# Layer 0's head and linear parts in another order, and two heads' maxima taken from neighbouring PSUM banks

## The chip, the cores and the metric

The kernel runs on one core of one Trainium2 chip. The metric is the device time of one execution in microseconds (us). The core has five engines with queues of their own: PE (TensorE, matmuls; PEld are its weight loads), DVE (VectorE), ACT (ScalarE), POOL (GpSimd) and SP (which issues most DMAs). The 16 KB of PSUM in each partition are eight banks of 512 fp32 numbers; PE writes its results there, and DVE and ACT read them.

## The reference

Two layers over x of 2 x 2048 tokens with 256 features. In each, x is normed, an attention-like part `s` and a feed-forward-like part `g` are computed from the normed x, and x becomes x + s * silu(g).

```
layer 0: s = linear attention(xn): rope, elu + 1 features, sums over all keys, W_out
         g = block(xn): layernorm, 16 causal heads of 16 with rope, Wproj, residual,
             layernorm, top-2 of 8 experts with capacity 1024, gelu, residual
layer 1: s = 16 causal heads of 16 + 16 (real and imaginary), Wo
         g = xn @ int4(kernel) + bias + (xn @ a) @ b
```

Softmax of the causal heads subtracts each row's maximum over the keys that the row may see.

## The kernel before

Tokens lie in tiles of 128 rows, 16 for each of two batch entries. The stages are a prelude (constants, loads), the attention of layer 0 with the linear attention and the routing to experts woven into it, the experts, and the attention of layer 1 with the rest of layer 1 woven in.

Heads are worked on in groups of four, eight groups per layer (two batch entries of four). The four heads of a group lie in four bands of 32 partitions, so that four score products run side by side, one in each band of rows of PE. For a group, pass A (`pass_a`) computes scores with queries in the rows, 128 queries by up to 512 keys, only for the row maxima; pass B (`pass_b`) computes them again with keys in the rows, after the maximum has been folded into the queries (layer 0, `subtract`) or added by a product (layer 1, `less_maximum`), and ACT takes the exponential (line 574) into `pt`. The value sums are products in column bands (line 804 in layer 0, line 1557 in layer 1). One step of the loop in `run_attention` takes one block of pass A and one of pass B for all four heads, in two halves of two heads each; a group has 40 blocks of pass A and 36 of pass B.

In pass A, a block that lies fully below the diagonal is reduced by DVE with a plain `tensor_reduce` (line 547). A block that holds the diagonal is reduced by a custom DVE instruction that adds a mask from the constants and takes the maximum (line 543). Each head has a bank and a reduction of its own. In pass B, the diagonal blocks get their mask by `hide` (line 505): four bf16 products of 32 rows, 256 columns wide, that add the mask `mask_h` in PSUM.

The order of the work is planned in Python, when the kernel is built, by the class `Plan`. The kernel declares steps with an engine, an estimated cost, the tiles read and written and a strand ("S" for the scores, "prep", "lin" and so on). Steps of one strand on one engine stay in order; a beam search chooses the order across strands by estimated times, and gives each PSUM tile one of the eight banks (the kind "s"). What is planned is emitted in that order, and the engines follow it with semaphores.

The names that follow in the text are these. `normalise0` norms four tiles of x: moments on DVE (`stats`, lines 476 and 478), a chain of small POOL instructions for the inverse roots (lines 481 to 488), scaling on ACT (line 696). `norm` scales a pair of tiles again for the block's own layernorm into `hn` (ACT, line 717), turns it on PE (line 360) and writes `ht` (DVE, line 721). `project` computes q, k and v of a tile (PE, line 736), copies them to `raw` (ACT, line 755), rotates them on POOL (lines 743 to 757), and after each second tile turns both (PE, line 764) and copies them to `qt` and `kt` (lines 770 and 772). `prepare` lists these parts for a group; the first group's are all declared before the loop, a later group's are spread over the loop's steps of the group before. The linear attention has `lin_keys` and `lin_out`, each over pairs of tiles (their products at lines 1066, 1117 and 1160, their rotation on POOL at lines 1039 to 1045); they fall due every 7.5 steps, from step 0 for the first batch entry and from step 180 for the second. `route` picks the experts and sends the rows on POOL (line 1000).

Of the kernel before, what the change touches and what calls it, by code (L numbers as in the profile page):

```python
# [17 lines left out]
P = 128  # L18
# [14 lines left out]
C_TRI = C_CAUSAL + 512  # L33
# [9 lines left out]
def _constants():  # L43
# [4 lines left out]
    c[:, C_CAUSAL + 384 : C_CAUSAL + 512] = np.where(r[None] <= r[:, None], 0.0, FAR)  # L48
# [23 lines left out]
class Buf:  # L72
# [3 lines left out]
    def __init__(self, kind):  # L76
        self.kind, self.n, self.uses, self.t = kind, None, 0, None
# [9 lines left out]
class State:  # L87


    def __init__(self, plan):  # L90
# [7 lines left out]
        self.since = {k: [0.0] * len(x) for k, x in plan.kinds.items()}  # L98
# [13 lines left out]
class Plan:  # L112
# [15 lines left out]

    GAP = 0.1
# [52 lines left out]
    def places(self, st, strand, s, t):  # L182

        take = []
        for b in s.bufs:
            if st.slot[b.n] is None:
# [3 lines left out]
                taken = [i for x, i in take if x.kind == b.kind]  # L190
                at, n = None, None
                for i, x in enumerate(st.since[b.kind]):
                    if x is not None and (at is None or x < at) and i not in taken:
                        at, n = x, i
# [6 lines left out]
    def advance(self, st, handicaps, until):  # L201
# [3 lines left out]
        while st.todo:  # L205
# [36 lines left out]
            for b, i in take:  # L242
                st.slot[b.n], st.since[b.kind][i] = i, None
                if b.kind == "s" and key[0] != "S":
                    st.guest[b.n] = key[0]
                    st.held[key[0]] = st.held.get(key[0], 0) + 1
# [18 lines left out]
            for b in s.bufs:  # L265
                st.left[b.n] -= 1
                st.until[b.n] = max(st.until[b.n], done)
                if st.left[b.n] == 0:
                    if st.guest[b.n]:
                        st.held[st.guest[b.n]] -= 1  # L270
                    st.since[b.kind][st.slot[b.n]] = st.until[b.n]
        return True

    def run(self):
# [36 lines left out]
        for s, take in order:  # L311
            for b, i in take:
                b.t = self.kinds[b.kind][i]()
# [5 lines left out]
def kernel(ctx: ExitStack, tc: tile.TileContext, i: dict, out: bass.AP):  # L319
# [15 lines left out]
    causal = cst[:, C_CAUSAL : C_CAUSAL + 512]  # L335
# [6 lines left out]
    def load_x(n):  # L342
        s = slice(n * NA // 4, (n + 1) * NA // 4)
        nc.sync.dma_start(xr[:, s], x_in[:, s])
# [32 lines left out]
    w0 = early.enter_context(tc.tile_pool(name="w0", bufs=1))  # L377
    prelude = ctx.enter_context(ExitStack())
# [6 lines left out]
    load_x(0)  # L385
# [4 lines left out]
    load_x(1)  # L390
# [4 lines left out]
    load_x(2)  # L395
    load_x(3)
# [4 lines left out]
    for n, c in enumerate((C_ID, C_AFTER)):  # L401
# [9 lines left out]
        if n == 0:  # L411
            nc.vector.tensor_copy(ident_h, m)
        else:
            nc.vector.tensor_copy(mask_h, m[:, :, None].to_broadcast([P, 4, 2, P]))
# [32 lines left out]
    def banks(ps, names):  # L447
        return [lambda n=n: ps.tile([P, 512], F32, tag=n, name=n, bufs=1) for n in names]
# [52 lines left out]
    def hide(out, j):  # L501

        r = slice(32 * j, 32 * j + 32)
        for q in range(4):
            nc.tensor.matmul(out, ident_h[r, q], mask_h[r, q].rearrange("p n k -> p (n k)"), start=False, stop=q == 3)  # L505
# [8 lines left out]
    def run_attention(plan, make, prepare, subtract, sum_keys, finish, last_sum, before=None, others=(), between=False):  # L514
# [16 lines left out]
        def pass_a(g, t, k, j, w, mx, parts):  # L531

            s, r, out = Buf("s"), slice(32 * j, 32 * j + 32), (mx, t, k, j)

            def score():
                nc.tensor.matmul(  # L536
                    s.t[:, :w], g.qt.t[r, t * P : (t + 1) * P], g.kt.t[r, 512 * k : 512 * k + w], start=True, stop=True
                )

            def largest():  # L540
                to = mx.t[:, t % 2, j, k : k + 1]
                if k == t // 4:
                    nc.vector.tensor_tensor_reduce(  # L543
                        s.t[:, :w], s.t[:, :w], causal[:, 512 - w :], 1.0, -3e38, ALU.add, ALU.max, to
                    )
                else:
                    nc.vector.tensor_reduce(to, s.t[:, :w], AX.X, ALU.max)  # L547

            keys = range(4 * k, 4 * k + -(-w // P))
            step = S("S", "PE", t_row(w), score, r=[(g.qt, t), *((g.kt, n) for n in keys)], w=[s], on=j)  # L550
            S("A", "DVE", t_dve(w) + (0.19 if k == t // 4 else 0.0), largest, r=[s], w=[out])
            parts.append(out)
            return step

        def pass_b(g, c, p, j, pt):
# [11 lines left out]
            def rest():  # L567
                if before:
                    S("S", "PE", 0.25 * t_row(w), before(g, c, j, s, w, not diagonal), r=[s, g.mh[c]], w=[s], on=j)
                if diagonal:  # L570
                    S("S", "PE", T_HIDE, lambda: hide(s.t[:, : 2 * P], j), r=[s], w=[s], on=j)
# [10 lines left out]
        for u in range(at + last_sum + 1):  # L582
# [11 lines left out]
            for i in (0, 2):  # L594


                more = []
                for x in range(2):
                    if a:
                        plan.pace = pass_a(g, t, k, i + x, wa, mx, parts)  # L600
                        first = first or plan.pace
                    if b:
                        step, rest, weigh = pass_b(gb, cb, p, (i + 2 + x) % 4, pt)
                        first = first or step
                        more.append((rest, weigh))
                for rest, _ in more:
# [36 lines left out]
    with ExitStack() as sc:  # L643
# [13 lines left out]
        for vt in vts:  # L657
            nc.vector.memset(vt, 1.0)
# [7 lines left out]
        nc.gpsimd.memset(ones, 1.0)  # L666
        outs = {}
# [3 lines left out]
                s=banks(ps, [f"s{n}" for n in range(8)]),  # L671
# [18 lines left out]
        def normalise0(n0):  # L690

            xs = [("xr", n0 + n) for n in range(4)]

            def scale():
                for n in range(n0, n0 + 4):
# [4 lines left out]
            stats("prep", n0, "r", ln_r, ln_m, ln_r1)  # L700
            S("prep", "ACT", 1.5, scale, r=[("r", n0)], w=xs)
# [9 lines left out]
        def norm(G, t):  # L711
# [14 lines left out]
            S("prep", "ACT", 0.75, shrink, r=[("xr", n0), ("xr", n0 + 1), ("r", n0 // 4 * 4)], w=[hn])  # L726
# [3 lines left out]
        def project(G, t):  # L730
# [27 lines left out]
            if t % 2:  # L758
                tp, at = Buf("s"), (t - 1) * P

                def turn():
                    for x in range(2):
                        for n in range(2):
                            nc.tensor.transpose(
# [939 lines left out]
```

## Time and profile before

| | |
|---|---|
| median of 3 runs (lowest, highest) | 3483.42 us (3477.35, 3490.22) |
| the profiled execution's own time, its span | 3508.01 us, 3506.2 us |
| busy share of the span: PE, PEld, DVE, ACT, POOL | 96%, 68%, 62%, 48%, 47% |
| mean granted TensorE clock | 0.97 |
| first score of layer 0, of layer 1 | 31.6 us, 2002.7 us |
| first product of the experts | 1505.28 us |

Rows of the profile name a line, an engine and an operation, the tile written and the tiles read, shapes as partitions x elements, a count, busy time and mean duration. Idle time is put down to the instruction that released the engine. Matmuls are pipelined and their ends are modelled, so that a busy PE is not PE at its peak; the starts of matmuls are the surer reading. An fp32 product is two matmul instructions.

### The profile page before, as it was taken

How to read it: one execution, taken by the hardware profiler on the slowest of the kernel's cores; microseconds unless marked ns; L12 is line 12 of the kernel's file. 1: busy time of each engine (PE TensorE's matmuls, PEld its weight loads, DVE VectorE, ACT ScalarE, POOL GpSimd, SP SyncE). 2: the span in 40 equal slices, each digit the busy share in tenths (PEclk: the TensorE clock that was granted, in tenths of full speed). 3: DMA queues.
4: the chain of work that ended last, by engine and by line, in shares of the span. 5: the costliest groups of instructions: out<-in, count | busy, mean ns of one | idle time of the engine just before them, and what ended most of it. 6: DMA issues, size and time to landing. Idle time of an engine off the chain costs nothing.

```text
span 3506.2 us, 81341 instructions
## 1 busy us (share of the span) xinstructions
PE 3350.0 (96%) x33814; PEld 2373.5 (68%) x33814; DVE 2163.6 (62%) x5599; ACT 1682.6 (48%) x3336; POOL 1660.5 (47%) x2223
## 2 busy tenths in 40 slices
PE   6999999999999999689989999999999999999998
PEld 4767777776777776456666556666776767777775
DVE  4777777777777877421121266667766657666774
ACT  3565555554555554311111265555445554554554
POOL 4443222323332221400000167989876657877877
PEclk7999999999999999789999999999999999999999
DMA  5000000000000000143333221010001010000000
GB/s 181 2 2 2 8 8 8 20 16 26 10 10 5 14 14 12 38 156 113 114 100 113 76 67 45 23 51 29 24 11 36 14 42 17 15 17 21 11 26 25
DMA packets 99508, 133.24 MB, mean 38 GB/s; under 512 B 9395, under 2 KB 76671, under 8 KB 99138
## 3 DMA queue, kind: packets, MB, share of 16 engines
q1 hardware_dynamic: 92994, 114.14, 10.1%
q0 software_dynamic: 6144, 13.88, 1.3%
q8 instruction: 266, 4.36, 0.5%
q14 instruction: 104, 0.85, 0.1%
HBM read 93.15 MB, written 37.75 MB: 37 GB/s over the span
## 4 chain that ended last, share of the span: by engine, by line
PE 45%; POOL 7%; DVE 2%; ACT 1%; issue 1%; DMA 1%; POOLq 0%; ACTq 0%; DVEq 0%
PE s L562 7%; PE s L536 7%; PE s L1347 6%; PE s L1341 6%; PE s L1557 6%; PE s L1468 3%; PE s L1526 2%; POOL ps L1542 2%; PE s L1563 2%; POOL ps L1543 2%; PE s L1605 2%; PE s L1483 1%; POOL ps L1538 1%; PE s L505 1%; PE s L1642 1%
## 5 line engine op out<-in xcount | busy, mean ns | idle before, releaser
L574 ACT ACTIVATE pt<-s 128x512 f32<-128x512 f32 (+1 forms) x2304 | 1168.9, 576 | 713.6 <-PE s L562 249.0
L562 PE MATMUL s<-qt,kt 32*128 32x256 f32 (+1 forms) x9216 | 1292.6, 388 | 7.9 <-ACT pt L574 4.4
L536 PE MATMUL s<-kt,qt 32*128 32x512 f32 (+3 forms) x5120 | 1269.7, 559 | 10.2 <-ACT pt L574 2.3
L547 DVE TENSOR_REDUCE mx<-s 128x1 f32<-128x512 f32 x1536 | 961.5, 682 | 185.0 <-PE s L536 101.9
L562 PEld LDWEIGHTS s<-qt,kt 32*128 32x128 f32 x9216 | 984.6, 185 | 62.0 <-ACT pt L574 16.2
L536 PEld LDWEIGHTS s<-kt,qt 32*128 32x128 f32 x5120 | 530.0, 186 | 170.0 <-issue 94.2
L543 DVE CUSTOM_DVE_ANT_0 s<-s,cst 128x128 f32<-128x128 f32 (+3 forms) x1024 | 482.3, 513 | 120.0 <-PE s L536 82.9
L1538 POOL TENSOR_TENSOR ps<-pt 128x1024 f32<-128x1024 f32 (+1 forms) x160 | 344.5, 2153 | 144.7 <-ACT pt L574 118.5
L743 POOL TENSOR_TENSOR ra<-raw,rope 128x128 f32<-128x128 f32 x128 | 58.6, 458 | 671.0 <-ACT raw L755 604.7
L1542 POOL TENSOR_TENSOR ps<-ps,pt 128x1024 f32<-128x1024 f32 x128 | 303.7, 2373 | 85.9 <-ACT pt L574 80.8
L1526 PE MATMUL s<-mh,ones_h 3*128 3x512 bf16 (+1 forms) x1152 | 317.3, 367 | 0.7 <-ACT mh L1519 0.7
L804 PE MATMUL s<-pt,vt 128*32 128x256 f32 (+1 forms) x4608 | 280.7, 381 | 5.3 <-issue 4.6
L1543 POOL TENSOR_TENSOR ps<-ps,pt 128x1024 f32<-128x1024 f32 (+1 forms) x128 | 269.2, 2103 | 10.0
L1557 PE MATMUL s<-pt,vt 128*32 128x256 f32 (+1 forms) x4608 | 271.3, 374 | 0.5 <-ACT pt L574 0.3
L1350 DVE TENSOR_TENSOR ye<-s,b 128x256 f32<-128x256 f32 x64 | 27.2, 424 | 391.6 <-PE s L1347 391.6
L1342 ACT ACTIVATE hm<-s,b1c 128x512 f32<-128x512 f32 x128 | 87.9, 687 | 359.6 <-PE s L1341 359.6
L1347 PE MATMUL s<-w,hm 128*128 128x256 f32 x1024 | 226.4, 382 | 8.5 <-ACT hm L1342 8.5
L1341 PE MATMUL s<-xt,w 128*128 128x512 f32 x512 | 226.4, 600 | 8.3 <-DVE xt L1282 8.3
L804 PEld LDWEIGHTS s<-pt,vt 128*32 128x32 f32 x4608 | 136.7, 112 | 135.0 <-issue 31.7
L1557 PEld LDWEIGHTS s<-pt,vt 128*32 128x32 f32 x4608 | 134.3, 110 | 136.4 <-DVE mx L547 18.0
L1347 PEld LDWEIGHTS s<-w,hm 128*128 128x128 f32 x1024 | 196.2, 192 | 42.9 <-ACT hm L1342 8.9
L505 PE MATMUL s<-mask_h,ident_h 32*128 32x256 bf16 x2048 | 197.7, 270 | 1.6 <-issue 1.6
(267 smaller groups left out, 4086.0 us busy)
## 6 DMA issues: line engine op xcount, KB each, us to landing
w<-in_L_ffn_W_dram SPq DMA_DIRECT2D x32, 1024.0 KB, 6.2
gl<-g_dram SPq DMA_DIRECT2D x64, 256.0 KB, 3.0
slots_in<-zero SPq DMA_DIRECT2D x8, 1024.0 KB, 10.2
xe<-slots_in SPq DMA_DIRECT2D x16, 512.0 KB, 8.0
slots_out<-ye SPq DMA_DIRECT2D x16, 512.0 KB, 7.2
xr<-in_L_attn_x_dram SPq DMA_DIRECT2D x4, 1024.0 KB, 5.6
s_dram<-lo SPq DMA_DIRECT2D x16, 256.0 KB, 2.0
hn<-in_L_attn_x_dram SPq DMA_DIRECT2D x16, 256.0 KB, 2.7
```

Of the source, the lines that this page charges most:

```text
L536: nc.tensor.matmul(s.t[:, :w], g.qt.t[r, t * P : (t + 1) * P], g.kt.t[r, 512 * k : 512 * k + w], start=True, stop=True)
L543: nc.vector.tensor_tensor_reduce(s.t[:, :w], s.t[:, :w], causal[:, 512 - w :], 1.0, -3e38, ALU.add, ALU.max, to)
L547: nc.vector.tensor_reduce(to, s.t[:, :w], AX.X, ALU.max)
L562: nc.tensor.matmul(s.t[:, at], g.kt.t[r, kj * P : (kj + 1) * P], g.qt.t[r, QC * c + q0 : QC * (c + 1)], start=n == 0, stop=n == 1 and not ...
L574: S("B", "ACT", t_act(w), lambda: nc.scalar.activation(pt.t[:, j, :w], s.t[:, :w], AF.Exp, scale=0.25), r=[s], w=[(pt, j)])
L804: nc.tensor.matmul(av.t[32 * j : 32 * j + 32, q0:QC], vts[G.vn][:, kj, j], pt.t[:, j, at], start=n == 0, stop=n == len(tiles) - 1,)
L1341: nc.tensor.matmul(ps, w1[:, k, f * P : (f + 1) * P], xt[:, k], start=k == 0, stop=k == 1)
L1347: nc.tensor.matmul(ps[:, :D], hm[:, f, s * P : (s + 1) * P], w2[:, f], start=f == 0, stop=f == FF // P - 1)
L1526: return lambda: nc.tensor.matmul(s.t[:, :w_], ones_h[r], G.mh[c].t[r, 512 - w_ :], start=False, stop=last)
L1538: nc.gpsimd.tensor_tensor(ps.t[:, :, q0:], pt.t[:, :, same], pt.t[:, :, odd], ALU.add)
L1542: nc.gpsimd.tensor_tensor(ps.t, ps.t, pt.t[:, :, even], ALU.add)
L1557: nc.tensor.matmul(av.t[32 * j : 32 * j + 32, q0:QC], G.vt.t[:, kj, j], pt.t[:, j, at], start=n == 0, stop=False)
```

## The change

Six edits come together.

1. In the head, x is loaded in pieces of 2, 2, 12 and 16 tiles, where it was four pieces of 8; `normalise0` takes the first four tiles in two chains of two. The ones in the two `vt` tiles are written by POOL (and only where they are needed), where DVE filled the whole tiles.
2. The turning of q and k leaves `project` for a part of its own, `turned_round`, which `prepare` puts behind the norming of the next pair.
3. The second batch entry's linear parts fall due from step 172, where it was 180.
4. Pass A takes two heads into two neighbouring banks, and one `tensor_reduce` takes both heads' maxima. All eight banks are one PSUM tile, and the planner gives a pair two banks that begin at an even one.
5. In layer 0 the diagonal blocks of pass A get their mask on PE: `hide` with a new bf16 mask `mask_q`, 128 columns wide, four products for each head, and then the joint plain reduction. In layer 1 they keep the custom instruction, head by head. `mask_q` is built in the prelude as the two other tables are; the fp32 mask of 512 columns shrinks to 128 in the constants, and layer 1 builds its own of 512 on POOL.
6. In layer 1 the tile `lt` is there once, where there were two.

```diff
-    load_x(0)
+    load_x(0, 2)
+    load_x(2, 4)
...
-    load_x(1)
+    load_x(4, 16)
...
-    for n, c in enumerate((C_ID, C_AFTER)):
+    for n, c in enumerate((C_ID, C_AFTER, C_CAUSAL)):
...
-    def hide(out, j):
+    def hide(out, j, mask):
         r = slice(32 * j, 32 * j + 32)
         for q in range(4):
-            nc.tensor.matmul(out, ident_h[r, q], mask_h[r, q].rearrange("p n k -> p (n k)"), start=False, stop=q == 3)
+            nc.tensor.matmul(out, ident_h[r, q], mask[r, q], start=False, stop=q == 3)
...
+            s, out, diagonal = Buf("s", True), (mx, t, k, i), k == t // 4
...
+            def products(x):
+                return S("S", "PE", t_row(w), lambda: score(x), r=[...], w=[(s, x)], on=i + x)
+
+            def rest():
+                for x in range(2) if diagonal and causal is None else ():
+                    S("S", "PE", T_HIDE / 2, lambda x=x: hide(s.t[:, x, w - P : w], i + x, mask_q), r=[(s, x)], w=[(s, x)], on=i + x)
+                if diagonal and causal is not None:
+                    for x in range(2):
+                        S("A", "DVE", t_dve(w) + 0.19, lambda x=x: nc.vector.tensor_tensor_reduce(
+                            s.t[:, x, :w], s.t[:, x, :w], causal[:, 512 - w :], 1.0, -3e38, ALU.add, ALU.max,
+                            mx.t[:, t % 2, i + x, k : k + 1],
+                        ), r=[(s, x)], w=[(*out, x)])
...
+                    return
+                S("A", "DVE", t_dve(2 * w), lambda: nc.vector.tensor_reduce(
+                    mx.t[:, t % 2, i : i + 2, k], s.t[:, :, :w], AX.X, ALU.max
+                ), r=[(s, 0), (s, 1)], w=[out])
...
+                if a:
+                    products, after_a = pass_a(g, t, k, i, wa, mx, parts)
                 for x in range(2):
                     if a:
-                        plan.pace = pass_a(g, t, k, i + x, wa, mx, parts)
+                        plan.pace = products(x)
...
+                if a:
+                    after_a()
...
-        for vt in vts:
-            nc.vector.memset(vt, 1.0)
+        for vt in vts:
+            nc.gpsimd.memset(vt[:, :, :, 16:], 1.0)
...
-                    if G.b == 0 and t % 4 == 0:
+                    if G.b == 0 and t == 0:
+                        parts.append(lambda: normalise0(0, 2))
+                        parts.append(lambda: normalise0(2, 2))
+                    elif G.b == 0 and t % 4 == 0:
                         parts.append(lambda t=t: normalise0(t))
                     parts.append(lambda t=t: norm(G, t))
+                if t:
+                    parts.append(lambda t=t - 2: turned_round(G, t))
                 for n in range(2):
                     parts.append(lambda t=t + n: project(G, t))
+            parts.append(lambda: turned_round(G, NT - 2))
...
-            start, every = ((0, 7.5), (180, 7.5))[b]
+            start, every = ((0, 7.5), (172, 7.5))[b]
```

In the planner, a pair is placed where both banks are free, from the time at which the later of them is:

```diff
-                for i, x in enumerate(st.since[b.kind]):
+                for i in range(0, len(since), 2) if b.pair else range(len(since)):
+                    x = since[i]
+                    if b.pair and x is not None:
+                        x = max(x, since[i + 1]) if since[i + 1] is not None else None
```

## The prediction

> **What bounds the kernel now.** I read the page's groups first, then a table of stretches cut where each head group's first score starts, then the timelines of the head, of TensorE and of the tail, then the waits.
>
> ```profile
> 207.70:370.50 162.80, 160.38 (x1808) 115.58 (x1804) 119.10 (x323) 92.07 (x197) 54.74 (x146) 0.97 0.01 2
> 370.50:530.20 159.70, 159.70 (x1884) 121.75 (x1880) 121.48 (x330) 92.51 (x192) 44.54 (x112) 1.00 0.02 8
> 1395.00:1505.00 110.00, 64.20 (x524) 46.70 (x516) 46.52 (x233) 34.79 (x70) 40.74 (x65) 0.74 0.23 76
> ```
>
> Columns: stretch, length, busy PE, PEld, DVE, ACT, POOL, granted clock, DMA share, GB/s. In a settled group of layer 0 (second row) PE is busy throughout and DVE three quarters. Busy PE is not full PE, so I looked at single steps, 4 heads of each pass:
>
> ```profile
> 310.73 0.69 PE L536 MATMUL s<-kt,qt 32*128 32x512 f32 x1
> 311.49 0.49 PE L505 MATMUL s<-mask_h,ident_h 32*128 32x256 bf16 x5
> 313.02 0.42 PE L804 MATMUL s<-pt,vt 128*32 128x256 f32 x4
> 503.66 0.69 PE L536 MATMUL s<-kt,qt 32*128 32x512 f32 x1
> 505.69 0.66 PE L764 MATMUL s<-cst,pad 128*128 128x128 f32 x4
> ```
>
> The step from 503.66 to 505.69 takes 2.03 us; the one from 310.73 to 313.02, whose pass B has mask products (L505) and 128 columns fewer, takes 2.29. Both run without a hole, and 237 of about 300 row stretches in this stage hold one whole step: PE sets the pace there. About 24 stretches hold two or three steps, and these wait for banks, which DVE and ACT empty:
>
> ```profile
> ACT pt L574 <- PE s L562: 247.1, 210, 5.1
> DVE mx L547 <- PE s L562: 64.8, 93, 3.4
> DVE s L543 <- PE s L536: 43.2, 63, 2.2
> PEld s L536 <- DVE mx L547: 11.9, 34, 0.8
> ```
>
> (waits of layer 0's attention: total us, times, longest.) DVE waits for PE much more than PE for DVE. The head is different:
>
> ```profile
> 10.27 1.76 DVE L658 MEMSET vt<- 128x2048 f32 x1 [0.37 <-DVE b1c L420]
> 14.10 1.34 DVE L476 BATCH_NORM_STATS2 ln_st<-xr 128x6 f32<-128x256 f32 x4
> 31.43 0.91 ACT L717 ACTIVATE hn<-xr,ln_n 128x256 f32<-128x256 f32 x2
> 51.33 0.91 ACT L717 ACTIVATE hn<-xr,ln_n 128x256 f32<-128x256 f32 x2 [0.91 <-POOL ln_n L466]
> 60.60 2.09 PE L536 MATMUL s<-kt,qt 32*128 32x512 f32 x8 [0.52 <-DVE qt L770]
> ```
>
> The first score starts at 31.59, and the steps of tiles 4 and 5 wait to 60.60: each pair is normed only after the pair before has been turned and copied.
>
> **The change, part by part** (minus is a gain).
>
> *Head.* A third mask in the prelude: 4 copies of 0.15 us, 8 matmul instructions of 0.23 (16 took 3.73), a cast of 0.69. PE's prelude ends 1.9 us later, and POOL's first memset, which waited for it at 8.85, starts at 10.7. POOL has 2.05 us of memsets and gets two more of 1024 columns (512 took 0.49, so 2.0 us); it is free at 14.7. Queued behind them is the first chain of roots, which started at 15.80 behind DVE's memsets (3.9 us, now gone) and four tiles' moments. With two tiles the chain is 5.5 us for 6.1 (the two-tile power in the tail takes 0.72 for 1.04): `hn` at 20.2 for 21.92. But the chain for tiles 2 and 3 now stands on POOL ahead of the first rotation: that can start at 25.7 for 26.49. First score about 0.8 us earlier. Pair 2 is then normed at 25.7 for 31.43; four rotations of 1.83 end at 33; the next chain, which ran from 45.0 to 51.1 behind a linear part's 4 us of rotation, ends at 39 to 43; the step of 60.60 comes 8 to 12 us earlier. From 95 us PE is busy 110.4 of 112.7, so what is won before that stays won. Check: group 0 takes 176.1 us, groups 1 and 2, with the same linear parts, 162.8 and 159.7, so 14.8 are there to win. I take -11; ends -16 and +2 (POOL's added memsets, nothing else). The small first loads put one more issue (0.6 us on SP) but half the bytes ahead of `wqkv`; POOL's memsets cover both, and uncovered it is that 0.6.
>
> *Maxima of layer 0.* 1024 custom instructions (half of them data, 512 heads) and 768 plain reductions become 256 + 384 joint ones. Four plain ones in a queue take 2.48 us, 0.60 each; custom ones queued take 0.25, 0.38, 0.51 and 0.65 by width, so 0.89 a pair. No joint one is in the trace. The rows of 256 and 512 columns read from PSUM (L813 417 ns, L1569 685 ns) give 149 ns and 1.05 ns a column, less 80 ns of overlap in a queue: 1.14 us for 1024 columns, 0.74 on average for the diagonal ones. Saved: 384 x 0.06 = 23 and 256 x 0.156 = 40, together 63 us of DVE. Since single-step stretches are PE's, I let a quarter come back: -16; ends 0 and -63.
>
> *Maxima of layer 1.* Only the plain ones are joined: 23 us of DVE, a quarter back: -6; ends 0 and -23. The custom ones still run one by one. Building `causal` costs POOL 0.5 us and a copy of 0.25 while PE norms the first tiles; uncovered, 0.8. One `lt` for two: gates are 8 or more parts apart, so no wait.
>
> *Masks of layer 0 on PE.* 512 heads x 4 products of 128 bf16 columns. The 256-column form starts every 0.107 us in its row group, two groups side by side (8 of them from 312.47 to 312.91), so 0.053 each if length decides and 0.107 if the load of weights does: 0.21 to 0.43 us a head, four heads side by side in 128 steps, 27 to 55 us. The two steps above differ by 0.26 where pure length says 0.21; I price a step at 0.26, the nearest row. Steps with 128 or 256 columns have cover: such a step needs 1.07 to 1.28 us of columns and takes at least 1.6 in the trace, waiting for banks. That leaves 64 steps: +17; without cover 128 x 0.26 = +33; ends 0 and +55.
>
> [...] No run here shows the 128-column form.
>
> *Banks.* A pair needs two adjacent free banks, and the first head's bank is held until the joint reduction ends, 0.54 us longer; the second's is free a little sooner. Bounds: nothing, or what the last rival says. I take 0, since one step's eight banks are exactly four pairs.
>
> *Order of turning in other groups, 24 parts for 16:* the same instructions and queues. 0.
>
> *Linear parts 8 steps earlier*, some 33 us. The last one now runs at 1444.7 to 1472.8, within the last two routes: its rotation holds POOL from 1452.10 to 1456.08, the sends come after it, and the last chain of roots starts at 1469.03 though its moments were ready at 1465.43. Moved with it are its rotations (POOL has 67.6 us of work in the 185.8 of group 4, so there is room), its loads of x on SP, and their one `hn` buffer, which group 4's norming may hold until step 174: the first part can lose the two steps, and the rest follow. I take 3.6 us plus some of its 5.9 us of PE: -5; ends -10 and +6 (the same PE work put where PE is full, nothing regained).
>
> *Sum:* -11 - 16 - 6 + 17 + 0 - 5 = -21 us. The profiled execution took 3508.0 (span 3506.2 and 1.8 around it), 24.6 above the median of the runs; I take the difference over: 3483 - 21 = 3462 (3487 under the profiler).
>
> **Rivals.** About 0.5%, 17 us, can be told from no change.
>
> 1. *DVE sets the pace.* For it: stretches of two or three steps take 4.75 us where columns and drain need 3.7, close to DVE's 4.8. Against: only 24 such stretches. Two thirds of the 86 us come back, -57 for -22: 3427. Chance 0.17.
> 2. *The masks eat it.* Nothing covers them: +33 for +17, and the sum is -5: 3478. For it: PE has no hole in 370 to 530 us. Chance 0.15.
> 3. *Pairs of banks (slower).* Prep, linear parts and value sums take single banks out of the pairs, so a pair waits for its second half while the first is empty. Place: the row stretches of both layers. For it: at 1081.9 us a step whose columns need 1.07 us takes 1.98, its second half starting as banks are released. If one step in five of the 640 loses 0.54 us, that is 69 us: 3531. It decides from 38 us on, 71 steps, one in nine. Against: rows and full products alternate, so most steps find empty banks. Chance 0.30.
>
> The forecast has 0.38.
>
> **Numbers.** Faster 0.38 + 0.17 = 0.55, same 0.15, slower 0.30. The range goes down to 3405 (rival 1 and the head's full 16, with some more on banks) and up to 3525 (masks at 55 with nothing from DVE is +39, so 3522, and a milder rival 3).
>
> **What would show it.** Right: first score near 31, and the step of tiles 4 and 5 near 50; group 0 near 165; no custom instruction in layer 0, joint rows of 1.2 us for 1024 columns; 128-column masks starting 0.053 to 0.08 us apart; the last linear part before 1450. Wrong: settled groups of layer 0 longer than 160 us with more PE waits behind L547's successor (rival 3), or the same length with a longer diagonal step (rival 2); layer 1 longer than its 1503 us would be rival 3 alone, for nothing else grows there.

## The result and the profile after

The kernel after takes 3468.99 us (median of 9 runs, 3464.54 to 3474.67), the kernel before 3485.58 (9 runs, 3477.35 to 3494.25): a ratio of 0.9954, 95% interval 0.9941 to 0.9967, or -16.6 us. A second comparison gave 0.9951 (0.9936 to 0.9967). The forecast was -21. Its total is right; the runs below show that most of its terms are not.

The profiled execution of after took 3473.7 us, 4.7 above its median; that of before, 3508.0, lay 24.6 above, and above each of the 37 timed runs of before in the comparisons that gave medians of 3485 to 3488 (the highest took 3494.25). So the two profiles differ by twice what the kernels do, and a stretch that is shorter than in before's profile need not be shorter by as much in a usual run. The stretches that answer to those shown of before (length, busy PE, PEld, DVE, ACT, POOL, clock, DMA share, GB/s):

```profile
205.50:363.40 157.90, 156.86 (x2073) 114.20 (x2069) 111.88 (x181) 92.06 (x198) 55.34 (x147) 1.00 0.01 2
363.40:526.90 163.50, 162.40 (x2146) 123.56 (x2142) 114.09 (x186) 93.33 (x193) 44.70 (x112) 1.00 0.03 8
1383.80:1461.90 78.10, 41.67 (x454) 30.19 (x446) 33.27 (x166) 25.08 (x53) 22.41 (x42) 0.77 0.27 91
```

In the second row, the settled group, DVE is busy for 114.09 us with 186 instructions where it had 121.48 with 330, yet the group is 163.5 us long where it was 159.7. Groups 5 and 6 of layer 0, counted from 0, grew alike (160.0 and 158.3 for 156.5 and 154.8). The stretch between layer 0's last score and the experts (third row) is 78.1 where it was 110.0.

The joint reductions and the new masks in after's groups by form (busy us, mean ns of one, idle before). Line numbers have moved: pass A's products are L548, its maxima L567, pass B's products L581, the masks L514.

```profile
L567 DVE TENSOR_REDUCE mx<-banks 128x2 f32<-128x1024 f32 x832 | 990.4, 1222 | 266.5 <-PE banks L548 131.7 <-PE banks L581 101.0 <-PE banks L514 25.2
L514 PE MATMUL banks<-mask_q,ident_h 32*128 32x128 bf16 x2048 | 109.4, 215 | 0.0
```

A joint reduction of 1024 columns takes 1.222 us in the mean (forecast 1.14; a plain one of 512 took 0.682 in before's mean). A step of 384 columns in TensorE's timeline of after (start, duration), in two halves, of which the first is shown with the start of the second:

```profile
506.15 0.58 PE L548 MATMUL banks<-kt,qt 32*128 32x384 f32 x1 [0.41 <-DVE mx L567]
506.90 0.21 PE L514 MATMUL banks<-mask_q,ident_h 32*128 32x128 bf16 x1
506.96 0.35 PE L514 MATMUL banks<-mask_q,ident_h 32*128 32x128 bf16 x6
507.29 0.58 PE L548 MATMUL banks<-kt,qt 32*128 32x384 f32 x1
```

The second half begins at 507.29, after the masks. In one row group they start at 506.903, 506.959, 507.015 and 507.071: 0.056 us apart with two row groups side by side, the low end of the forecast's 0.053 to 0.107.

The waits of layer 0's attention in after (total us, times, longest):

```profile
ACT pt L593 <- PE banks L581: 196.5, 182, 3.8
DVE mx L567 <- PE banks L581: 138.1, 177, 2.8
DVE mx L567 <- PE banks L514: 47.9, 56, 3.9
PEld banks L548 <- DVE mx L567: 21.2, 66, 0.8
```

DVE's maxima now wait some 215 us for TensorE's scores and masks (the two rows and 28.6 behind L548), where those of before had 147 (64.8 and 29.5 for the plain, 42.3 and 10.8 for the custom ones): DVE was relieved, and the relief became waiting. TensorE's weight loads for pass A wait 21.2 us for the maxima, where they had 11.9 behind the plain and 3.8 behind the custom ones; all its weight loads together wait 36 us for maxima in both kernels. The head, in after's timeline:

```profile
10.27 0.74 DVE L485 BATCH_NORM_STATS2 ln_st<-xr 128x6 f32<-128x256 f32 x2
11.78 1.84 POOL L689 MEMSET vt<- 128x1024 f32 x2
19.24 0.20 POOL L475 TENSOR_TENSOR ln_n<-ln_n,ln_t 128x2 f32<-128x2 f32 x1
22.26 1.09 ACT L721 ACTIVATE xr<-xr,ln_m,ln_r 128x256 f32<-128x256 f32 x2 [4.34 <-POOL ln_m L493]
23.25 0.89 ACT L743 ACTIVATE hn<-xr,ln_n 128x256 f32<-128x256 f32 x2
```

The first root is ready at 19.44, but `hn` starts at 23.25, because ACT's queue holds the scaling of tiles 2 and 3 (22.26) ahead of it, and that waits for the second chain on POOL. The first score is at 34.0, not 31, and the step of tiles 4 and 5 starts at 49.0 (60.6 before). A second profile of after has 32.0 and 47.2.

### The profile page after: what moved, and what is told of

Same layout as the page of the kernel before. It is cut to its first block, busy times and chain, and to the rows that moved or that the text cites. A ratio compares the mean times of both kernels' runs of the same rounds, so it can differ in the third digit from the quotient of the medians.

```text
span 3471.9 us, 84289 instructions
## 1 busy us (share of the span) xinstructions
PE 3326.3 (96%) x35870; PEld 2332.2 (67%) x35870; DVE 2078.6 (60%) x4066; ACT 1678.3 (48%) x3336; POOL 1667.2 (48%) x2242
## 4 chain that ended last, share of the span: by engine, by line
PE 44%; POOL 8%; DVE 2%; ACT 2%; issue 2%; DMA 1%; POOLq 0%; DVEq 0%; ACTq 0%
PE banks L548 7%; PE banks L581 6%; PE s L1381 6%; PE s L1375 6%; PE banks L1594 6%; PE banks L1505 3%; POOL ps L1579 2%; POOL ps L1580 2%; PE banks L1563 2%; PE banks L1600 2%; PE banks L1520 1%; POOL ps L1575 1%; PE banks L1642 1%; PE banks L514 1%; ACT pt L593 1%
## 5 line engine op out<-in xcount | busy, mean ns | idle before, releaser
L593 ACT ACTIVATE pt<-banks 128x512 f32<-128x512 f32 (+1 forms) x2304 | 1165.7, 575 | 713.2 <-PE banks L1563 211.0
L567 DVE TENSOR_REDUCE mx<-banks 128x2 f32<-128x1024 f32 (+3 forms) x1024 | 1121.1, 1122 | 344.5 <-PE banks L581 153.3
L581 PE MATMUL banks<-qt,kt 32*128 32x256 f32 (+1 forms) x9216 | 1247.3, 388 | 8.2 <-DVE mx L567 5.3
L548 PE MATMUL banks<-kt,qt 32*128 32x512 f32 (+3 forms) x5120 | 1239.9, 560 | 11.3 <-DVE mx L567 5.1
L581 PEld LDWEIGHTS banks<-qt,kt 32*128 32x128 f32 x9216 | 935.2, 186 | 44.9 <-ACT pt L593 11.0
L548 PEld LDWEIGHTS banks<-kt,qt 32*128 32x128 f32 x5120 | 486.2, 185 | 205.5 <-issue 111.8
L769 POOL TENSOR_TENSOR ra<-raw,rope 128x128 f32<-128x128 f32 x128 | 60.6, 474 | 540.4 <-ACT raw L781 497.4
L1563 PE MATMUL banks<-mh,ones_h 3*128 3x512 bf16 (+1 forms) x1152 | 299.5, 371 | 0.0
L561 DVE CUSTOM_DVE_ANT_0 banks<-banks,causal 128x384 f32<-128x384 f32 (+3 forms) x512 | 242.4, 514 | 56.8 <-PE banks L548 43.1
L1594 PE MATMUL banks<-pt,vt 128*32 128x256 f32 (+1 forms) x4608 | 275.5, 377 | 0.7 <-ACT pt L593 0.5
L832 PE MATMUL banks<-pt,vt 128*32 128x256 f32 (+1 forms) x4608 | 268.0, 371 | 1.5 <-DVE mx L567 0.9
L1594 PEld LDWEIGHTS banks<-pt,vt 128*32 128x32 f32 x4608 | 135.5, 111 | 141.3 <-ACT pt L593 37.2
L514 PEld LDWEIGHTS <-ident_h 32*128 32x128 bf16 x4096 | 200.0, 93 | 29.6 <-issue 15.1
L832 PEld LDWEIGHTS banks<-pt,vt 128*32 128x32 f32 x4608 | 133.4, 109 | 116.8 <-issue 16.9
```

The lines of the kernel that those rows point to most:

```text
L548: nc.tensor.matmul(s.t[:, x, :w], g.qt.t[r, t * P : (t + 1) * P], g.kt.t[r, 512 * k : 512 * k + w], start=True, stop=not (diagonal and cau ...
L567: S("A", "DVE", t_dve(2 * w), lambda: nc.vector.tensor_reduce(mx.t[:, t % 2, i : i + 2, k], s.t[:, :, :w], AX.X, ALU.max), r=[(s, 0), (s, ...
L581: nc.tensor.matmul(s.t[:, at], g.kt.t[r, kj * P : (kj + 1) * P], g.qt.t[r, QC * c + q0 : QC * (c + 1)], start=n == 0, stop=n == 1 and not ...
L593: S("B", "ACT", t_act(w), lambda: nc.scalar.activation(pt.t[:, j, :w], s.t[:, :w], AF.Exp, scale=0.25), r=[s], w=[(pt, j)])
L832: nc.tensor.matmul(av.t[32 * j : 32 * j + 32, q0:QC], vts[G.vn][:, kj, j], pt.t[:, j, at], start=n == 0, stop=n == len(tiles) - 1,)
L1563: return lambda: nc.tensor.matmul(s.t[:, :w_], ones_h[r], G.mh[c].t[r, 512 - w_ :], start=False, stop=last)
```

## The half clock, which the forecast left out

The granted clock falls to 0.50 at times, in layer 0's groups for 3.4 to 17.1 us (the longest in before, from 49.2 to 66.3 us). The kernel before in stretches of 1 us (the same columns, the clock third from the end):

```profile
265.00:266.00 1.00, 0.00 (x0) 0.00 (x0) 0.26 (x1) 0.00 (x0) 1.00 (x2) 1.00 0.00 0
267.00:268.00 1.00, 1.00 (x5) 0.48 (x4) 1.00 (x3) 1.00 (x4) 0.70 (x3) 0.83 0.00 0
268.00:269.00 1.00, 1.00 (x4) 1.00 (x4) 1.00 (x2) 1.00 (x3) 0.00 (x0) 0.50 0.00 0
277.00:278.00 1.00, 1.00 (x12) 0.20 (x4) 0.00 (x0) 0.00 (x0) 0.00 (x0) 0.55 0.00 0
```

TensorE is idle from 264.9 to 266.8 us and then, from 267.7, has half the clock for 10.2 us: a hole of 1.9 us is followed by a loss of about 5 more. In before's layer 0 six such stretches begin between 70 and 1390 us. The other five (from 677, 735, 804, 855 and 1363 us, 6.8 or 10.2 us long) begin in a route's sends or up to 2.5 us after their end, eight indirect DMAs on POOL in 10.0 to 15.8 us. Two of those in POOL's timeline of before:

```profile
673.68 0.97 POOL L1000 DMA_INDIRECT slots_in<-x,to  x1 [0.30 <-issue]
674.95 0.97 POOL L1000 DMA_INDIRECT slots_in<-x,to  x1 [0.30 <-issue]
```

And the stretches of 4 us around them:

```profile
668.00:672.00 4.00, 4.00 (x44) 2.67 (x46) 3.86 (x17) 1.77 (x4) 3.09 (x4) 1.00 0.41 146
672.00:676.00 4.00, 3.07 (x31) 1.61 (x24) 0.04 (x1) 0.69 (x2) 3.01 (x4) 1.00 0.33 118
676.00:680.00 4.00, 2.93 (x13) 2.11 (x14) 1.51 (x3) 0.87 (x2) 3.21 (x8) 0.66 0.18 66
```

In 672 to 677 TensorE has four gaps, up to 0.91 us, that are put to "issue", and DVE and ACT starve with it. After's profile has none of these stretches in layer 0 between 70 and 1390 us, though its sends are as long (10.0 to 15.8 us for the first five).

The length of a hole doesn't decide it alone. Two runs of the table below, after without edit 5 and the same with layer 1 unpaired, have the same hole in layer 0; in the first the clock stays full, in the second it is halved for 6.8 us. First TensorE's next product and a stretch of 2 us in the one, then in the other:

```profile
778.23 0.66 PE L367 MATMUL banks<-cst,x 128*128 128x128 f32 x4 [2.62 <-ACT pt L594]
778.00:780.00 2.00, 1.77 (x13) 1.65 (x14) 0.79 (x3) 2.00 (x7) 0.10 (x1) 1.00 0.00 0
778.37 0.90 PE L367 MATMUL banks<-cst,x 128*128 128x128 f32 x3 [2.61 <-ACT pt L609]
778.00:780.00 2.00, 1.63 (x8) 1.63 (x9) 0.64 (x2) 2.00 (x6) 0.00 (x0) 0.50 0.00 0
```

Each run's time can be split in two: what the clock took, span x (1 - mean granted clock), and the rest. While the clock is halved TensorE also waits at times (in before it does nothing from 58 to 59 us, at 0.50), so the first is an upper bound. Means over all runs of a kernel, before in the same comparison:

| kernel | median us | ratio to before (95%) | clock took | rest |
|---|---|---|---|---|
| before / after | 3487.9 / 3468.9 | 0.9951 (0.9936 to 0.9967) | 88.7 / 69.3 | 3397.8 / 3399.0 |
| before + edits 1, 2 | 3442.1 | 0.9882 (0.9864 to 0.9901) | 69.6 | 3375.0 |
| after without edit 5 | 3460.9 | 0.9930 (0.9916 to 0.9944) | 76.1 | 3385.2 |
| same, layer 1 unpaired | 3459.7 | 0.9923 (0.9909 to 0.9938) | 77.8 | 3382.1 |
| before, beside the next four | 3485.1 | 1 | 94.9 | 3390.5 |
| before + edit 2 | 3473.6 | 0.9966 (0.9952 to 0.9979) | 81.9 | 3390.0 |
| before + edits 1, 2, 3 | 3449.1 | 0.9895 (0.9878 to 0.9911) | 71.0 | 3377.2 |
| before, other seed | 3506.8 | 1.0072 (1.0057 to 1.0086) | 99.4 | 3409.7 |
| before + edits 1, 2, other seed | 3482.9 | 0.9997 (0.9988 to 1.0005) | 86.4 | 3397.2 |

By the first row after gains 19 us of clock, and the rest is the same to about 2 us. That isn't yet a cause. Before itself moves by 6 to 7 us in both columns from one comparison to the next (88.7 and 94.9, 3397.8 and 3390.5), and the loss isn't all in places where TensorE is the bound. By stage, from the clocks of the two profiles: layer 0's groups lose 36.1 us before and 6.8 after, layer 1 18.4 and 27.9, and the stretch ahead of the experts 28.3 and 17.9. In that stretch TensorE is busy for little more than half of the time (64.20 of 110.0 us before, 41.67 of 78.1 after), so its loss falls by 10 simply because it is shorter. The rest hides two changes too: at full clock layer 0's groups take 16 us more than before (1343 for 1327), the stretch ahead of the experts 22 less (60 for 82).

## The experiments

Theory A named the causes from the two traces: the earlier linear parts bring most, the masks cost some 27 us, layer 1's pairs of banks cost 13. Theory B: every edit makes the planner find another order, and its luck decides. Theory C, after the first four runs: the half clock.

**First four.** They ran on another chip, on which before took 3515.59 us; each has its ratio to that.

*Edit 3 alone:* `((0, 7.5), (180, 7.5))[b]` becomes `((0, 7.5), (172, 7.5))[b]` in before.

> The kernel before with edit 3 alone: the second entry's linear parts fall due from step 172 instead of 180. Theory A (the earlier linear parts bring the gain): in the two traces the stretch from the last score of layer 0 to the experts' first product went from 110.3 to 78.1 us, -32, and the groups that now hold the parts lose some of it; expected 3460 to 3470, -15 to -25, with that stretch near 80 us. The prediction's own term was -5 (-10 to +6), the stretch near 105. Theory B (the order that the planner happens to find, and a profiled execution of before that lay 22 us above its median, make the difference): within 5 us of before, the stretch anywhere, and the groups of layer 0 moved by amounts that follow no edit.

3517.55 us, ratio 1.0013 (1.0004 to 1.0023): 4.6 us slower. Group 7 in before's profile, then here with the stretch ahead of the experts:

```profile
1217.80:1395.00 177.20, 174.30 (x1866) 131.15 (x1866) 133.05 (x379) 96.61 (x194) 35.48 (x72) 0.97 0.04 13
1232.60:1419.40 186.80, 178.74 (x1900) 133.11 (x1896) 137.38 (x403) 100.69 (x200) 39.80 (x76) 0.96 0.05 15
1419.40:1513.60 94.20, 50.08 (x465) 36.38 (x459) 39.66 (x203) 28.13 (x59) 32.90 (x57) 0.72 0.23 79
```

The stretch did shrink, from 110.0 us, but group 7 grew by 9.6 us and group 4 from 185.8 to 193.1. The tail of layer 0 is no place to read a gain from: what left it (15.8 us) turned up in the groups (9.6 and 7.3). Theory A falls here.

*Edit 3 undone in after:* the same line the other way.

> The kernel after with edit 3 undone: the second entry's linear parts fall due from step 180 again. Theory A: the stretch between layer 0's last score and the experts' first product back from 78 to 105 to 110 us, and the whole 15 to 25 us slower than after (3484 to 3494). The prediction's term: 5 us slower than after. Theory B: within 5 us of after, either side.

3514.58 us, 1.0008 (0.9995 to 1.0021). After itself didn't run on that chip, so this number decides nothing alone. But the split run below did, with edit 3 and after's planned order, and has 0.9988: beside it, undoing edit 3 costs 7 us by the ratios (4.5 by the medians), with intervals of some 4 us on each, and all of it in the rest (3424.3 for 3417.4), not in the clock. That is the forecast's sign. Group 3, at full clock in after's two profiles (183.8 and 183.9 us), has a half-clock stretch here at 704 us, in a route's sends, and takes 193.1; in the split run it takes 193.1 too. So these stretches seem to hang on the chip as well.

*Masks twice:* the same planned order, and so no draw in it.

```diff
-    def hide(out, j, mask):
+    def hide(out, j, mask, times=1):
...
-        for q in range(4):
-            nc.tensor.matmul(out, ident_h[r, q], mask[r, q], start=False, stop=q == 3)
+        for n in range(4 * times):
+            q = n % 4
+            nc.tensor.matmul(out, ident_h[r, q], mask[r, q], start=False, stop=n == 4 * times - 1)
```

Pass A's masks call it with `times` 2.

> The kernel after, but each mask of pass A in layer 0 is added twice: eight products of 128 columns for each head instead of four, in the same planned order. It measures what one set of masks costs where it stands. The prediction's term: 64 steps without cover at 0.26 us, +17, so 3486; with no cover at all 128 steps at 0.26, +33, 3502. From the steps of after's trace (+0.43, +0.22, +0.2 and 0 us for steps of 512, 384, 256 and 128 columns, four of each in a group) 27 us: 3496. If DVE's reductions or the banks set the pace of these steps, under 8 us: below 3477.

3593.26 us, 1.0216 (1.0193 to 1.0239): some 80 us above the two other variants of after on that chip (3514.58 and 3510.05), far beyond all three figures. Read at full clock, in the table of stretches, groups 5 and 6 of layer 0:

```profile
947.00:1116.00 169.00, 168.67 (x2337) 124.25 (x2333) 111.91 (x175) 89.92 (x195) 49.20 (x120) 1.00 0.03 8
1116.00:1284.00 168.00, 167.31 (x2366) 129.30 (x2362) 112.55 (x181) 90.90 (x189) 45.42 (x112) 1.00 0.04 11
```

The same two in after's second profile:

```profile
878.40:1038.40 160.00, 158.93 (x2082) 113.61 (x2078) 111.71 (x175) 89.40 (x195) 49.04 (x120) 1.00 0.03 8
1038.40:1196.60 158.20, 157.31 (x2110) 117.88 (x2106) 112.42 (x180) 90.23 (x188) 45.41 (x112) 1.00 0.04 12
```

A second set costs 9.0 and 9.8 us a group (9.0 and 8.4 in groups 1 and 2), some 0.6 us for each of 16 steps: two halves, four more products of 0.056 us in each, is 0.45; what the remainder is isn't shown. In these groups, where TensorE is busy for 168.67 of 169.00 and 167.31 of 168.00 us, the second set was paid in full and a little over.

*Joint reductions split:* two plain ones in place of each joint one, banks and planned order kept.

```diff
-                S("A", "DVE", t_dve(2 * w), lambda: nc.vector.tensor_reduce(
-                    mx.t[:, t % 2, i : i + 2, k], s.t[:, :, :w], AX.X, ALU.max
-                ), r=[(s, 0), (s, 1)], w=[out])
+                def maxima():
+                    for x in range(2):
+                        nc.vector.tensor_reduce(mx.t[:, t % 2, i + x, k : k + 1], s.t[:, x, :w], AX.X, ALU.max)
+
+                S("A", "DVE", t_dve(2 * w), maxima, r=[(s, 0), (s, 1)], w=[out])
```

> The kernel after, with the pairs of banks and the planned order kept, but each joint reduction written as two plain ones, a head each, in both layers. DVE's work grows by some 71 us (640 full pairs at 0.06 and 256 diagonal pairs at 0.1, in layer 0 and 1 together). The prediction let a quarter of saved DVE work come back: +18, 3487. If DVE is slack (60% busy in after's profile): within 4 us of after. If DVE sets the pace wherever a row stretch holds more than one step: +35 or more, 3505.

3510.05 us, 0.9988 (0.9979 to 0.9997), on the slower chip, with half-clock stretches in groups 3, 4 and 7 that after's profile lacks. At full clock, the same two groups in the table of stretches of this kernel:

```profile
902.70:1062.10 159.40, 159.05 (x2082) 114.17 (x2078) 116.44 (x255) 89.22 (x195) 49.26 (x120) 1.00 0.03 8
1062.10:1220.10 158.00, 157.55 (x2110) 118.92 (x2106) 116.59 (x260) 90.05 (x188) 45.56 (x112) 1.00 0.04 12
```

DVE has 4.7 and 4.2 us more to do and 80 instructions more; the groups are 0.6 and 0.2 us shorter. Over the nine groups of both layers that ran at full clock in both kernels (1521.2 us in after's first profile, 1518.2 here) nothing is lost either. The joining of two reductions in itself brings nothing there; the custom instruction, which the joint one replaced on the diagonal, isn't tested by this run.

**Second four**, on one chip.

*After again.*

> The kernel after itself, beside the runs of before that the next three share, with a second profile. The recorded comparison gave a ratio of 0.9954. Theory C, formed from the first four runs: PE's holes of about 2 us trip the granted clock to a half for some 10 us each (in before's trace a hole from 264.9 to 266.8 us is followed by 0.50 until 277), and where such holes fall differs from plan to plan and from run to run. By C the settled groups repeat to a microsecond and the count of half-clock stretches in layer 0 between 60 and 1390 us (six in before's profile, none in after's) is what moves: some now, and the group that has one is about 5 us longer. If the gain is the edits' alone: the ratio 0.995 again and the stretches none.

3468.86 us, 0.9951. The settled groups repeat to 0.1 us. No half-clock stretch in layer 0 between 60 and 1390 us, as in the first profile; the chip of the first four runs gave after's variants three or four.

*After without edit 5:* `causal` again from the constants, also for layer 0, and no `mask_q`.

```diff
...
-        run_attention(plan, Group0, prepare, subtract, sum_keys, finish, SUM_LAG0, others=others, between=True)
+        run_attention(plan, Group0, prepare, subtract, sum_keys, finish, SUM_LAG0, others=others, between=True, causal=causal)
...
```

> The kernel after with edit 5 undone: layer 0's diagonal blocks of pass A go back to the custom instruction on DVE, head by head, with no mask products on PE; the pairs of banks, the joint reductions of the full blocks, the head and the linear parts stay as in after. By the prediction's terms: masks gone -17, the 40 us of DVE work that the diagonal blocks saved come back by a quarter, +10: 7 us faster than after, ratio to before 0.993. By the steps of after's trace (27 us of masks, a sixth of DVE's work on the path as the split run gave): 20 us faster, 0.990. By the doubled masks (a second set cost 2.6%): 60 to 90 us faster, 0.970 to 0.978. If the masks are covered: 10 us slower than after, 0.998.

3460.91 us, 0.9930: 8 us faster than after, as the forecast's terms have it (7), not the 20 of the trace's steps nor the 60 of the doubled masks. The rest falls by 14 us, and the clock takes 7 more. Group 2, in the table of stretches, is 157.5 us long, where after has 163.5:

```profile
353.40:510.90 157.50, 157.25 (x1880) 119.15 (x1876) 117.33 (x277) 91.74 (x191) 45.61 (x112) 1.00 0.02 9
```

Group 5 falls from 160.0 to 154.9 us, group 6 rises from 158.2 to 160.9, and the stretch ahead of the experts from 78.5 to 95.8. In this draw of the plan edit 5 is a loss.

*The same, and layer 1 unpaired:* each head a `Buf("s")` of its own and a plain reduction there.

> As the run before it, and in layer 1 each head has a bank and a plain reduction of its own again, as in the kernel before; layer 0 keeps its pairs of banks. Theory A: layer 1 took 1467.0 us from first to last score in after's trace and 1453.7 in before's, with 70 more changes between row, full and column products, so unpaired it is 13 us shorter: 13 us faster than the run before it. The prediction's term: the joint maxima of layer 1 brought 6, so 6 us slower. Theory B (the plan's luck): layer 1 as in before's trace to a few us, since its plan alone is what differs.

3459.74 us, 0.9923, 1.2 us from the run before it. Layer 1's last five groups take 880.4 us unpaired and 881.6 paired. Its first three take 580.6 and 582.1 us, with 19.7 and 16.0 of these lost to the clock. Neither 13 faster nor 6 slower: layer 1's joint maxima have no effect that this comparison can tell.

*Edits 1 and 2 alone, on before.*

> The kernel before with edits 1 and 2 alone (loads, ones on POOL, two chains of two tiles, turning behind the next pair's norming), without a third mask in the prelude. The prediction's term: -11, 3.2 parts in a thousand (0.9968), the step of tiles 4 and 5 8 to 12 us earlier, first score 0.8 us earlier or better, since the third mask isn't there. From the two traces: groups 0 and 1 4.8 us shorter each, so -7 to -10. Theory B: any sign within 10 us, because the plan of the whole of layer 0 is made anew.

3442.11 us, 0.9882: 41 us faster than before, 27 faster than after. Its first score is at 33.0, the step of tiles 4 and 5 at 46.8, and group 0 ends at 199.0, where it ended at 207.7: 8.7 us won in the head, near the forecast's 11. But the most came later. Groups 3 and 4, in which the second entry is normed and turned, in before's table of stretches (the profile that lies 24.6 us above the median):

```profile
530.20:720.70 190.50, 188.05 (x1996) 141.62 (x1992) 139.45 (x407) 105.72 (x221) 51.74 (x126) 0.97 0.04 13
720.70:906.50 185.80, 179.94 (x1886) 129.05 (x1882) 140.94 (x423) 98.55 (x210) 67.61 (x154) 0.94 0.06 21
```

And here:

```profile
512.60:693.50 180.90, 180.90 (x2008) 139.24 (x2004) 140.69 (x411) 106.89 (x224) 53.97 (x132) 1.00 0.04 13
693.50:858.20 164.70, 164.63 (x1860) 122.47 (x1856) 135.98 (x417) 95.89 (x204) 65.66 (x147) 1.00 0.07 24
```

31 us shorter, 17 of them clock (190.5 x 0.03 + 185.8 x 0.06). That is against the long profile of before: the two profiles differ by 66 us, the medians by 46, so a usual run of before may lose less here. The same kernel with edit 3 alone, profiled near its median on the other chip, has these stretches too (0.97 and 0.94 in these groups).

**Last four**, on one chip.

*Edits 1, 2 and 3, on before.*

> The kernel before with edits 1, 2 and 3 (the run with edits 1 and 2 alone gave 0.9882, some 41 us faster than before; with edits 1 to 4, layer 1's pairs left out, 0.9923). It tells whether edit 3 or layer 0's pairs of banks gives those 14 us away. If the pairs do: 0.988 again or the prediction's -5 beside it, 0.987. If the earlier linear parts do: near 0.992. Theory B (every plan is a draw): anywhere from 0.985 to 0.997.

3449.1 us, 0.9895: 4.5 us slower than with edits 1 and 2, within both intervals, and as edit 3 alone had it (+4.6). The step from here to 0.9923 is layer 0's pairs of banks together with edit 6, about +10, with intervals of 6 us on each side. In the two profiles 5.6 of 13.4 us of it lie in layer 1, where both kernels have single banks.

*Edit 2 alone, on before.*

> The kernel before with edit 2 alone: turning behind the norming of the next pair, in every group, and nothing else. The prediction put the whole of it into the head (part of -11) and 0 into later groups. From the traces of before and of the run with edits 1 and 2: groups 3 and 4, in which the second entry is normed and turned, went from 376.3 to 345.6 us, and half-clock stretches from 16.8 us lost to none. If edit 2 does that: 25 to 35 us faster (0.990 to 0.993), with groups 3 and 4 near 345. If it is the head alone: at most 11 faster (0.997), groups 3 and 4 near 376. Theory B: these two groups anywhere between.

3473.62 us, 0.9966: 12 us faster. Groups 3 and 4 take 179.4 and 171.0 us (350.4 for 376.3), both at a clock of 1.00. The first of them in the table of stretches:

```profile
522.50:701.90 179.40, 179.40 (x1992) 138.63 (x1988) 139.69 (x408) 105.45 (x223) 54.76 (x132) 1.00 0.04 13
```

By the table it is the clock, which takes 13.0 us less; the rest is the same to 0.5. The place was expected, the size (25 to 35) was not: these two groups are 26 us shorter than in before's long profile, the kernel only 12 faster.

*Before with another seed:* `random.Random(0)` becomes `random.Random(1)`.

> The kernel before with another seed in the planner's draws (1 for 0); no edit at all. It measures what a plan made anew is worth by itself. Theory A (the edits decide): within 5 us of before, 0.9986 to 1.0014. Theory B (luck): 10 to 20 us to either side, with other holes in PE and other half-clock stretches, and layer 1, too, a few us different.

3506.82 us, 1.0072: 25 us slower by the ratio with no edit at all, 19 of them in the rest. Layer 1 takes 1471.3 us from first to last score where it took 1453.7; its first group alone takes 218.1 for 199.6, with 17 us lost to the clock in this profile.

*Edits 1 and 2 with that seed.*

> Edits 1 and 2 on the kernel before, with the other seed. If the 41 us of these two edits are theirs, this run lies 35 to 45 us below the run of before with the same seed; if they were a lucky draw, 10 to 20 us below it (the prediction's 11 and some half-clock stretches).

3482.88 us: 0.9997 / 1.0072 = 0.9926 of the run before it, 26 us faster, half of it clock (13.0) and half the rest (12.5). It lies between the two expectations. Both draws show a gain above the forecast's 11; its size is 41 in one and 26 in the other.

## Why the total was right and the terms were not

From before to after in steps, each ratio x 3486 us:

| step | forecast | measured |
|---|---|---|
| edits 1 and 2 | -11 | -41 (other seed -26) |
| edit 3 | -5 | +4.5 (alone +4.6; in after's order, beside the split run, -7) |
| edit 4 in layer 0, full blocks and banks, with edit 6 | -6 | +10 |
| edit 4 in layer 1 | -6 | +2.5 |
| edit 5, masks +17, diagonal reductions -10 | +7 | +7 |
| sum | -21 | -17 |

(The -16 for layer 0's maxima was a quarter of 23 us for full blocks and of 40 for diagonal ones. The measured steps add up to the total of the second comparison because each is the difference of two runs in a row.) The misses, -30, +9.5, +16 and +8.5, cancel to 4 us. That is luck.

*Head: smaller than forecast in its own place, and the step that failed is "the order of turning in other groups: 0".* By the end of group 0 edits 1 and 2 had won 8.7 us (5.7 with the other seed), after 2.2 and 7.4 in its two profiles, for 11. Turning alone brought 12 us, by the table all of it clock; in its profile groups 3 and 4 have none of the half-clock stretches of before's. With edit 1 beside it, 12 to 23 us of the rest go besides, and where is not shown. The head's own first step was wrong in sign (first score 0.4 to 2.4 us later in after's two profiles: POOL's queue was followed, ACT's was not), the second right (49.0 and 47.2 for "near 50"). Group 0 took 171.5 and 168.3 us in the two profiles for "near 165".

*"A quarter of the saved DVE work comes back": refuted for the joining of two reductions.* None does. The prediction had the reason in hand (single-step stretches are TensorE's) and granted the quarter all the same.

*Masks: the sum with the diagonal reductions holds, the terms aren't shown.* Edit 5 costs 7 to 8 us in all for +7, in one draw. The forecast's 0.107 us between starts of the 256-column form is 0.109 in before's trace, which changes little. But the masks are dearer than 0.26 us where nothing covers them (2.87 us for 2.29 in a step of 512 columns whose pass B has its mask too, 2.47 for 2.03 without), steps of 256 columns, which the prediction took as covered, need 2.08 to 2.15 us for 1.81, and only those of 128 are nearly free (in the median 1.84 us for 1.86 without a mask in pass B, 2.29 for 2.33 with one). By such steps the masks cost 27 us, and a second set cost 8.4 to 9.8 in each settled group. If that is right, dropping the custom instruction brought more than the 10, and two errors cancel. The settled groups did come out longer than 160 us (163.5), the prediction's sign for rival 3. Without edit 5 two of the three that are shown fall back by 5 to 6 us and one rises, so the masks are the likelier cause.

*Linear parts: no gain shown.* Two comparisons have +4.5 where -5 was forecast, one has -7. The 3.6 us of the last rotation and chain were read off the tail; what the same products cost in groups 4 and 7 was put only at the range's end.

*Rival 3, pairs of banks:* layer 1 took 1514 us from its first score for 1503 (1510 in after's second profile), which the prediction named as its mark, "for nothing else grows there". Something else does: the clock took 27.9 and 24.3 us of it for 18.4, and at full clock layer 1 takes 1486.3 and 1486.0 for 1485.1. The unpaired run, too, takes 1511. Layer 0's +10 may be the pairs; one draw can't tell, since another seed alone moves the kernel by 25 us. For the same reason the +4.5, the +2.5 and edit 5's +7 are no verdicts; the split reductions, the doubled masks and the gain of edits 1 and 2 with two seeds are.

*What stays open:* why TensorE has gaps that are put to "issue" during a route's sends in some runs and not in others, why one hole halves the clock and its like doesn't, which of edit 1's three parts brings its share, what edit 6 does, and edit 3's sign. Before with edits 1 and 2, 3442 us, is the fastest of these kernels.

## What to carry to other kernels

Look at the granted clock stretch by stretch before pricing an edit: here a 1.9 us hole in a busy TensorE was followed by a loss of 5 us more, and by the split the whole gain of turning later was clock (13.0 us, in a kernel 12 faster). But ask of each loss whether TensorE was the bound in that place. Here the joining of reductions on DVE, which already waited 147 us for TensorE in layer 0, brought nothing (nine groups took 1521.2 us with it and 1518.2 without), while a second set of masks on TensorE, which set the pace, was paid in full (9.0 and 9.8 us a group). When a planner makes the order anew, one build per edit is one draw: measure the spread with another seed, and test single terms with the order kept. A profile that lies far above the median is no measure for a stretch.

## What was not expected of the hardware

After a hole of 1.9 us the clock was halved for 10.2. Shorter ones were followed by 0.50 too: at 672 to 677 us, gaps of at most 0.91 us, 1.8 us together. But after holes of 2.62 us (above) and 3.27 us (at 2334.9 us with edits 1 and 2) the clock stayed at 1.00, so these runs show no length from which it falls. One chip ran the kernel before 0.8% slower than the others did (3515.59 for 3485 to 3488), with 7 to 14 us more taken by the clock and 14 to 22 us more in the rest.
